# First layer of a four-layer network: where the next image's rows are scaled, and one slot's shift in the layer norm

## Chip, cores and metric

One core of one Trainium2 chip runs the whole program. The metric is the device time of one execution in microseconds (us), lower is better; the number for a kernel is the median over its runs. A profiled execution on the same core gives the trace from which all durations below come. The engines are named as the profile names them: PE (TensorE, with PEld for its weight loads), DVE (VectorE), ACT (ScalarE), POOL (GpSimd), and SP, whose queue issues nearly all DMAs.

## What is computed

The reference is four layers, each added to its input after a group norm. The change is in the first one, a two-dimensional selective scan (4 images of 64 x 64 pixels, 128 channels, inner width 256, 16 states, 4 scan directions). Cut to what matters:

```python
x = x + ss2d(group_norm(x))                      # layer 0, then three other layers
# ss2d:
xh, z = split(x @ in_proj_w.T)                   # 256 channels each
xc = silu(depthwise_conv3x3(xh) + conv_b)        # per image
for k in 4 directions:                           # rows, columns, and both reversed
    delta = softplus(dt_proj(x_proj(xc)));  B, C = x_proj(xc)
    h[t] = exp(delta[t] * A) * h[t-1] + delta[t] * u[t] * B[t]     # 16 states
    y += sum_n h[n] * C[n]
y = layer_norm(y over 256 channels) * silu(z)
out = y @ out_proj_w.T
```

The group norm of the input is a scale and an offset for each channel; the kernel applies them to the rows of the image ahead of the convolution (the scaling that the change moves). The layer norm over the 256 channels is `y * nb + mb` with `nb` the reciprocal deviation and `mb = -mean * nb`.

## The kernel before

**Units and slots.** Layer 0 is one long hand-ordered loop (lines 656 to 779). A unit is one image `b` (4), one direction `k` (4) and one chunk `c` of 512 pixels (8): 128 units. A unit has 16 slots, one for each state `n`: 2048 slots in all. In each slot the program emits, in this order:

- POOL: `dB = du * B` for both halves of the channels (line 699, 128 x 1024)
- DVE: what is filed under `"dve"` for this slot, then for each of the two halves ACT's `dA = exp(delta * A)` (line 704) and DVE's scan over 512 pixels (line 705)
- PE: eight transposes of the scanned `h` of seven slots ago (line 549), and the products of the slot before (line 584); ACT: the copy `hT` out of PSUM (line 559)
- ACT: what is filed under `"act2"` for this slot
- PE and POOL: steps of the next unit by `TABLE`; among them, `delta` on DVE at the head of slots 9 and 11 (line 484), and on POOL `du0` after slot 10's dB and `du1` after slot 12's (line 487)

The order of PE, ACT, DVE and POOL is the order of emission (`tc.manual_schedule`); that of the SP queue is left to the framework. dB has three buffers, so POOL may be up to about two slots ahead of DVE; dA has three PSUM buffers, and the transposes' PSUM tile `pt` has one.

**Work on the side.** While the scans of image `b` run, generators prepare image `b+1` (`before`, line 305) and finish image `b-1` (`after`, line 367). Each `yield` names a kind of piece. At the end of every slot the loop steps pieces whose kind may stand in this slot (`SIDE`) and whose turn has come (`due`). `later(place, f, slots=m)` (line 643) files an operation to be emitted `m` slots on, at `place`.

`before` takes the rows of an image in 8 chunks. For each: `gates` (two products for `z`), then two convolutions `s = 0, 1` of nine matmuls, one in each slot from slot 11 to slot 3 of the next unit. So a chunk takes three units, and I call them A (s = 0 starts in its slot 11), B (s = 0 ends in slot 3, s = 1 starts in slot 11) and C (s = 1 ends in slot 3). The next chunk's rows are loaded at the first matmul of s = 0 and scaled in place by `scaled` (line 324): one ACT instruction, 128 x 10 x 64 values, filed at the sixth matmul of s = 1 for one slot on, which is slot 1 of a C unit. The first chunk of an image is scaled before the loop over the chunks starts. There are 24 scalings (3 images, 8 chunks).

`after` normalises a chunk of an earlier image. For the first two images (`b + 2 < NB`, that is while the scans of images 1 and 2 run) the piece `"t"` emits `nb` on ACT at once, files `mb` (4 columns, DVE, line 390) two slots on, and four operations of 128 x 256 on ACT (`yf`, line 393) two to five slots on. `"t"` may stand in slots 11, 12, 15 and 0, and stands in slot 12 of a B unit in all 16 cases; so `mb` is emitted ahead of slot 14's scans and the four operations at the end of slots 14, 15, 0 and 1. `free_at = slot + 6` holds the next piece, the transposes of the normalised rows, until they are through. For images 2 and 3 DVE does the norm in another way, which isn't touched. Helpers carry the line of the filed call: in the profile `mb`, `yf` and other filed operations stand under L645.

Of the kernel before, what the change touches and what calls it, by code (L numbers as in the profile page):

```python
# [12 lines left out]
AF = mybir.ActivationFunctionType  # L13
ALU = mybir.AluOpType
# [10 lines left out]
NCH = NT // CH  # L25
# [57 lines left out]
def layer0(sh, A, x_in, x_out, scr, ahead):  # L83
# [6 lines left out]
    tc, nc = sh.tc, sh.nc  # L90
    with ExitStack() as ctx:
# [60 lines left out]
        def conv(xn, s, bank, out):  # L152

            for t in range(9):
                yield "c"
                if t == 0:
                    pm = bank("cv")
                dy, dx = divmod(t, 3)
                nc.tensor.matmul(  # L159
                    pm,  # L160
                    lhsT=taps[:, s, t, :],
                    rhs=xn[:, dy : dy + 8, dx : dx + 64],
                    start=(t == 0),
                    stop=(t == 8),
                )
            out.append(pm)
# [6 lines left out]
        def gates(b, c, v, bank, later, es=(None, None)):  # L173
            for s in range(2):
                yield "z"
                zp = bank("zp")
                nc.tensor.matmul(zp, lhsT=w_in[:, 2 + s, :], rhs=v, start=True, stop=True)
                silu(zp, 0.0, 0.0, scr(f"z{b % 3}")[s, :, c * CH : (c + 1) * CH], later, (("act0", 2), ("act0", 3), 4), es[s])
# [126 lines left out]
        def before(b, bank, later):  # L305

            st = small.tile([P, NCH, 6], F32, name="gn_st")
            for c in range(NCH):  # L310
                yield "l"
                t = tmp.tile([P, CH], F32, name="xs", tag="t2", bufs=4)
                nc.sync.dma_start(t.rearrange("p (h w) -> p h w", w=64), A["x_t"][b, :, 8 * c + 1 : 8 * c + 9, 1:65])
                yield "s"
                later("dve", nc.vector.bn_stats, st[:, c, :], t)
            yield "m"
            s_, o_ = sh.group_scale(st, psm, small, "m", exp_rstd)

            def load(c):
                xn = tmp.tile([P, 10, 66], F32, name="xn", bufs=3)  # L320
                nc.sync.dma_start(xn, A["x_t"][b, :, 8 * c : 8 * c + 10, :])
                return xn

            def scaled(xn, c, r0, r1):
                inner = xn[:, max(r0, int(c == 0)) : min(r1, 10 - int(c == NCH - 1)), 1:65]
                nc.scalar.activation(inner, inner, AF.Identity, scale=s_, bias=o_)

            yield "l"
            ahead = load(0)
            yield "x"  # L330
            later("act2", scaled, ahead, 0, 0, 10)
            for c in range(NCH):
                xn = ahead
                yield from gates(b, c, xn[:, 1:9, 1:65], bank, later)
                for s in range(2):
                    for t, piece in enumerate(conv(xn, s, bank, out := [])):
                        yield piece
                        if c < NCH - 1 and (s, t) == (0, 0):
                            ahead = load(c + 1)
                        if c < NCH - 1 and s == 1 and t == 5:  # L340
                            later("act2", scaled, ahead, c + 1, 0, 10)
                    grown(b, c, s, out[0], later)

        def silu(v, bias, minus, dst, later, wait, e=None):
# [22 lines left out]
        def after(b, st, later, bands):  # L367

            for c in bands:
                yield "l"  # L370
                rows = slice(c * CH, (c + 1) * CH)
                if kept:
                    y = kept.pop()
                else:
                    y = tmp.tile([P, 4, 2 * P], F32, name="yf", tag="t4", bufs=4)
                    nc.sync.dma_start(y, tiles(scr(f"y2{b % 2}")[rows, :]))
                z = tmp.tile([P, 2, CH], F32, name="zf", tag="t4", bufs=4)
                nc.sync.dma_start(z, scr(f"z{b % 3}")[:, :, rows].rearrange("s p t -> p s t"))
                mv = small.tile([P, 4, 2], F32, name="ln_mv")
                for q in range(4):  # L380
                    nc.vector.bn_aggr(mv[:, q, :], st[:, 4 * c + q])

                rs = small.tile([P, 4], F32, name="ln_r")
                later("act1", nc.scalar.activation, rs, mv[:, :, 1], AF.Ln, bias=sh.eps5)
                if b + 2 < NB:
                    yield "t"
                    nb = small.tile([P, 4], F32, name="nb")
                    nc.scalar.activation(nb, rs, AF.Exp, scale=-0.5)
                    mb = small.tile([P, 4], F32, name="mb")
                    later("dve", nc.vector.scalar_tensor_tensor, mb, mv[:, :, 0], -1.0, nb, ALU.mult, ALU.mult, slots=2)  # L390
                    for q in range(4):
                        norm = dict(scale=nb[:, q : q + 1], bias=mb[:, q : q + 1])
                        later("act2", nc.scalar.activation, y[:, q, :], y[:, q, :], AF.Identity, slots=2 + q, **norm)
                else:
                    yield "n"

                    nb = spare("nb")[:, 0:4]
                    nc.scalar.activation(nb, rs, AF.Exp, scale=-0.5)
                    for q in range(4):
                        later("dve", normed, y[:, q, :], mv[:, q, 0:1], nb[:, q : q + 1])  # L400
                yg = tmp.tile([P, 2, CH], F32, name="yg", bufs=2)
                for s in range(2):
                    yield "m"
                    pt = spare("pg")
                    for q in range(4):
                        nc.tensor.transpose(pt[:, q * P : (q + 1) * P], y[:, q, s * P : (s + 1) * P], sh.ident)
                    norm = dict(scale=on_w[:, s : s + 1], bias=on_b[:, s : s + 1])
                    later("act0", nc.scalar.activation, yg[:, s, :], pt, AF.Identity, **norm)
                yield "f"
                xr = tmp.tile([P, 4, DM], F32, name="xr", tag="t2", bufs=4)  # L410
                nc.sync.dma_start(xr, tiles(x_in(b)[rows, :]))
                if b < NB - 1 or c > 2:
                    yield "g"
                nc.gpsimd.tensor_tensor(yg, yg, z, ALU.mult)
                if b + 2 < NB:
                    yield "o"
                    op = psy.tile([P, 2, 2 * P], F32, name=f"yT{int(not rev)}").rearrange("p r d -> p (r d)")
                else:
                    yield "m"
                    op = spare("op")  # L420
                op = op.rearrange("p (q d) -> p q d", q=4)
                for q in range(4):
                    for s in range(2):
                        nc.tensor.matmul(
                            op[:, q, :], lhsT=yg[:, s, q * P : (q + 1) * P], rhs=w_out[:, s, :], start=(s == 0), stop=(s == 1)
                        )
                later("dve", residual, b, rows, xr, op, slots=2)
# [134 lines left out]
        def products(G, q, hT):  # L562
# [68 lines left out]
            c={11},  # L631
            g={7},
            s={11, 12, 13, 14, 15, 0, 1, 2, 3},
            t={11, 12, 15, 0},
            o={8},
            f=(),
            l=(),
# [3 lines left out]
        slot = 0  # L641

        def later(place, f, *a, slots=1, **kw):

            todo.setdefault((slot + slots, place), []).append(lambda: f(*a, **kw))  # L645
# [10 lines left out]
        with tc.manual_schedule(engines=order):  # L656
# [4 lines left out]
            for i, (b, k, c) in enumerate(units):  # L661
# [25 lines left out]
                for n in range(NS):  # L687
                    slot = NS * i + n
                    g, q = divmod(n, 4)
# [39 lines left out]
                    if n == 10:  # L729
                        y = unit["y"] = tmp.tile([P, 4, 2 * P], F32, name="y", tag="t4", bufs=4)  # L730
# [15 lines left out]
                        d.step()  # L746
                    for d in sides:
                        if d.need == "t" and n in SIDE["t"] and d.due(slot) and (inside or not any(o.taps for o in sides)):
                            d.free_at = slot + 6
                            d.step()  # L750
                        if d.need == "o" and n in SIDE["o"] and d.due(slot - 8):
                            d.step()
                        if d.need == "s" and n in SIDE["s"] and d.due(slot):
                            d.step()
                        if d.need in ("f", "l") and d.due(slot):
                            if d.need == "l":
                                d.free_at = slot + 3
                            d.step()
# [1455 lines left out]
```

## Time and profile before

| What | Value |
|---|---|
| median of 3 runs (lowest, highest) | 7645.87 us (7638.12, 7647.14) |
| the profiled execution: time | 7645.85 us |
| its span, first to last instruction | 7644.1 us |
| first scan to last scan of layer 0 | 112.8 to 5591.8 us, 2048 slots of 2.68 us |
| scan, L705 (DVE) | 4096 of 1266 ns |
| dB, L699 (POOL) | 2048 of 2387 ns |
| dA, L704 (ACT) | 4096 of 696 ns |
| hT, L559 (ACT) | 2048 of 1016 ns |
| scaling, L326 (ACT) | 24, median 924 ns |
| mb, L645 (DVE) | 16, median 1432 ns |
| yf, L645 (ACT) | 64, median 603 ns |

How to read it: a row of the profile names the line, the engine, the operation, what it writes and reads with sizes, the count, and the mean time of one. Consecutive instructions of DVE and ACT overlap by about 0.1 us, so that the distance from start to start, not the duration, is what one costs its engine. In a time line the first two columns are start and length in us, and "[0.32 <-PE pt L549]" means that the engine sat idle for 0.32 us before it and that PE's write of pt released it.

### The profile page before, as it was taken

To read this page: it belongs to the slowest core of one execution; us is meant where nothing else is said; L and a number is where in the kernel's file an instruction comes from. 1 tells how busy PE (TensorE), PEld (TensorE's weight loads), DVE (VectorE), ACT (ScalarE), POOL (GpSimd) and SP (SyncE) were. 2 spreads that over 40 slices of the span, in tenths; PEclk is the share of its full clock that TensorE was granted. 3 is DMA by queue.
4 is the path that set the end of the run, shared out by engine and by line. 5 is a ranking of instruction groups with operands and counts; after the bars stand their busy time and mean duration, and the time that the engine had idled before them with its cause. 6 is when DMAs were issued, how large, how long until landed. Compare 5 with 4: busy or idle time off the path is not lost.

```text
span 7644.1 us, 140402 instructions
## 1 busy us (share of the span) xinstructions
PE 6293.8 (82%) x52604; PEld 3973.6 (52%) x52604; DVE 6715.7 (88%) x7999; ACT 6135.0 (80%) x9771; POOL 5691.9 (74%) x2688
## 2 busy tenths in 40 slices
PE   7888888778898877888887777787789978686889
PEld 3554444444455544445554444454467756464556
DVE  7999999999999999999999999999956655656678
ACT  7999999999999999999999999999943323324667
POOL 4999999999999999999999999999920024123233
PEclk8999999999999999999999999999999988788999
DMA  6656566546667554565756445555533241331332
GB/s 181 171 177 176 182 175 180 171 154 178 198 180 195 184 179 160 167 196 178 183 191 180 165 169 180 179 185 174 190 92 73 59 120 46 83 99 46 102 95 82
DMA packets 1328925, 1160.66 MB, mean 152 GB/s; under 512 B 718709, under 2 KB 1119697, under 8 KB 1261298
## 3 DMA queue, kind: packets, MB, share of 16 engines
q1 hardware_dynamic: 1323970, 1149.24, 50.4%
q8 instruction: 414, 6.78, 0.4%
q10 hardware_dynamic: 4272, 2.43, 0.1%
q14 instruction: 269, 2.20, 0.1%
HBM read 958.19 MB, written 189.21 MB: 150 GB/s over the span
## 4 chain that ended last, share of the span: by engine, by line
ACT 36%; PE 31%; DVE 18%; issue 8%; POOL 3%; DMA 2%; SPq 1%; ACTq 0%; DVEq 0%; POOLq 0%
ACT hT L559 14%; ACT dA L704 14%; DVE h L705 12%; PE pt L549 5%; PE cv L159 3%; POOL dB L699 3%; PE yT L584 3%; PE pf L939 2%; PE po L952 1%; ACT e L645 1%; ACT delta L478 1%; PE yT L458 1%; PE pz L1183 1%; PE pt L1892 1%; ACT delta L481 1%
## 5 line engine op out<-in xcount | busy, mean ns | idle before, releaser
L705 DVE TENSOR_TENSOR_SCAN h<-dA,state,dB 128x512 f32<-128x512 f32 x4096 | 4927.0, 1266 | 120.7 <-ACT dA L704 72.4
L699 POOL TENSOR_TENSOR dB<-du,Bb 128x1024 f32<-128x1024 f32 x2048 | 4816.5, 2387 | 152.3 <-DVE h L705 118.2
L549 PE MATMUL pt<-ident,h 128*128 128x128 f32 x16384 | 2216.7, 278 | 859.2 <-ACT hT L559 833.8
L704 ACT ACTIVATE dA<-delta,A_neg 128x512 f32<-128x512 f32 x4096 | 2765.5, 696 | 102.7 <-DVE h L705 77.0
L549 PEld LDWEIGHTS pt<-ident,h 128*128 128x128 f32 x16384 | 1802.7, 141 | 1917.7 <-ACT hT L559 1700.5
L559 ACT COPY hT<-pt 128x1024 f32<-128x1024 f32 x2048 | 2080.7, 1016 | 125.5 <-PE pt L549 105.9
L584 PE MATMUL yT<-hT,W 128*32 128x256 f32 x16384 | 1378.6, 409 | 4.3 <-DVE xr L433 3.5
L584 PEld LDWEIGHTS yT<-hT,W 128*32 128x32 f32 x16384 | 456.2, 150 | 346.3 <-issue 324.3
L159 PE MATMUL cv<-xn,taps 128*128 128x512 f32 x936 | 527.1, 645 | 2.7 <-DVE delta L484 2.6
L1183 POOL TENSOR_TENSOR xg<-xg,so 128x1024 f32<-128x1024 f32 x16 | 39.3, 2469 | 622.8 <-PE pu L1183 622.2
L1930 POOL TENSOR_TENSOR S<-S,sm 128x784 f32<-128x784 f32 x128 | 191.1, 1493 | 416.3 <-DVE sm L1928 250.0
L487 POOL TENSOR_TENSOR du<-delta,u 128x512 f32<-128x512 f32 x256 | 327.8, 1281 | 163.6 <-DVE delta L484 162.2
L475 PE MATMUL dp<-xd,w_dt 65*128 65x512 f32 x512 | 288.7, 646 | 33.8 <-DVE delta L484 23.7
L458 PE MATMUL yT<-u,w_x 128*48 128x512 f32 x508 | 244.4, 604 | 21.3 <-DVE y L600 20.1
L1937 ACT ACTIVATE S<-S,mx 128x196 f32<-128x196 f32 x512 | 227.9, 448 | 33.2 <-DVE mx L1964 32.7
L159 PEld LDWEIGHTS cv<-xn,taps 128*128 128x128 f32 x936 | 139.2, 188 | 180.5 <-issue 160.4
L940 ACT ACTIVATE h<-pf,b 128x512 f32<-128x512 f32 x128 | 87.6, 687 | 118.8 <-PE pf L939 100.5
L484 DVE SCALAR_TENSOR_TENSOR delta<-delta,dp 128x512 f32<-128x512 f32 x256 | 169.7, 663 | 3.2 <-ACT delta L481 1.0
L1183 POOL TENSOR_TENSOR WX<-wr,Xs 128x544 f32<-128x544 f32 x40 | 59.3, 1483 | 149.1 <-issue 63.4
L1892 PE MATMUL pt<-ident,S 128*98 128x128 f32 x1024 | 165.6, 286 | 3.5 <-POOL S L1930 2.0
L481 ACT ACTIVATE delta<-delta 128x512 f32<-128x512 f32 x256 | 164.5, 643 | 0.0
L478 ACT ACTIVATE delta<-dp 128x512 f32<-128x512 f32 x256 | 152.3, 595 | 10.4 <-PE dp L475 9.2
(381 smaller groups left out, 6921.7 us busy)
## 6 DMA issues: line engine op xcount, KB each, us to landing
Bb<-l_B SPq DMA_DIRECT2D x512, 1024.0 KB
W<-l_W SPq DMA_DIRECT2D x512, 256.0 KB
l_y<-y SPq DMA_DIRECT2D x127, 512.0 KB
u<-l_xr SPq DMA_DIRECT2D x64, 512.0 KB
u<-l_xw SPq DMA_DIRECT2D x64, 512.0 KB
y<-l_y SPq DMA_DIRECT2D x56, 512.0 KB
V<-l_v SPq DMA_DIRECT2D x512, 49.0 KB
y<-l_y SPq DMA_DIRECT2D x80, 256.0 KB
```

The source lines that it names most:

```text
L159: nc.tensor.matmul(pm, lhsT=taps[:, s, t, :], rhs=xn[:, dy : dy + 8, dx : dx + 64], start=(t == 0), stop=(t == 8),)
L458: nc.tensor.matmul(bank["x"], lhsT=w_x[:, s, k, :], rhs=u[:, s, :], start=(s == 0), stop=(s == 1))
L475: nc.tensor.matmul(bank[s], lhsT=w_dt[:, k, s * P : (s + 1) * P], rhs=xd, start=True, stop=True)
L481: nc.scalar.activation(delta[:, s, :], delta[:, s, :], AF.Ln, bias=1.0)
L487: nc.gpsimd.tensor_tensor(du[:, s, :], delta[:, s, :], u[:, s, :], ALU.mult)
L549: nc.tensor.transpose(pt[:, j, s, :], G["h"][:, s, t0 : t0 + 32, :].rearrange("p t n -> p (t n)"), sh.ident)
L559: return lambda: nc.scalar.copy(hT, pt.rearrange("p j s d -> p j (s d)"))
L584: nc.tensor.matmul(U["yT"][e][32 * jo : 32 * jo + 32, qo % 2, :], lhsT=U["Ws"][G["g"]][:, :, 4 * q + j], rhs=hT[:, j, :], start=((e, jo) n ...
L699: nc.gpsimd.tensor_tensor(dB, du, B_now[:, q : q + 1, :].to_broadcast([P, 2, CH]), ALU.mult)
L704: nc.scalar.activation(dA, delta[:, s, :], AF.Exp, scale=A_neg[:, k, s, n : n + 1])
L705: nc.vector.tensor_tensor_scan(h[:, s, :, q], dA, dB[:, s, :], state[:, s, n : n + 1], ALU.mult, ALU.add)
L1892: nc.tensor.transpose(pt[:, half, hp, :], U["S"][:, e, hp, 98 * half : 98 * half + 98], sh.ident)
```

## The change

The scaling of rows becomes a `tensor_scalar` (multiply, then add) on POOL, and for all chunks but the first it is filed at the last matmul of s = 0 for five slots on: slot 8 of a B unit, emitted on POOL's queue between the dB of slot 8 and that of slot 9. `mb` is filed three slots after `"t"` in place of two (ahead of slot 15's scans), and the four `yf` operations three to six slots after it (slots 15, 0, 1 and 2). `"t"` may stand in slot 12 alone, and the piece after it waits for seven slots.

```diff
             def scaled(xn, c, r0, r1):
                 inner = xn[:, max(r0, int(c == 0)) : min(r1, 10 - int(c == NCH - 1)), 1:65]
-                nc.scalar.activation(inner, inner, AF.Identity, scale=s_, bias=o_)
+                nc.gpsimd.tensor_scalar(inner, inner, s_, o_, ALU.mult, ALU.add)
...
-                        if c < NCH - 1 and s == 1 and t == 5:
-                            later("act2", scaled, ahead, c + 1, 0, 10)
+                        if c < NCH - 1 and s == 0 and t == 8:
+                            later("act2", scaled, ahead, c + 1, 0, 10, slots=5)
...
-                    later("dve", nc.vector.scalar_tensor_tensor, mb, mv[:, :, 0], -1.0, nb, ALU.mult, ALU.mult, slots=2)
+                    later("dve", nc.vector.scalar_tensor_tensor, mb, mv[:, :, 0], -1.0, nb, ALU.mult, ALU.mult, slots=3)
                     for q in range(4):
                         norm = dict(scale=nb[:, q : q + 1], bias=mb[:, q : q + 1])
-                        later("act2", nc.scalar.activation, y[:, q, :], y[:, q, :], AF.Identity, slots=2 + q, **norm)
+                        later("act2", nc.scalar.activation, y[:, q, :], y[:, q, :], AF.Identity, slots=3 + q, **norm)
...
-            t={11, 12, 15, 0},
+            t={12},
...
-                            d.free_at = slot + 6
+                            d.free_at = slot + 7
```

## The prediction, made before the changed kernel ran

> **What bounds the kernel now.** I read in this order: the page, the busy time by stage, the waits of the stage, and then the time line around the edited instructions. The first layer takes 5.6 of the 7.64 ms, and the edits act only while scans of images 0, 1 and 2 run (about 125 to 4300 us), because only then is a next image prepared (line 326) or an earlier one normalised by ScalarE (lines 386 to 393).
>
> ```profile
> PE 6293.8 (82%) x52604; PEld 3973.6 (52%) x52604; DVE 6715.7 (88%) x7999; ACT 6135.0 (80%) x9771; POOL 5691.9 (74%) x2688
> ```
>
> ```profile
> 500.00:1300.00 800.00, 685.39 (x5220) 388.10 (x5212) 783.55 (x717) 773.98 (x1115) 753.52 (x341) 1.00 0.65 181
> 1700.00:2600.00 900.00, 788.70 (x6023) 458.97 (x6016) 871.57 (x812) 875.98 (x1281) 846.18 (x384) 1.00 0.65 186
> ```
>
> The columns are PE, PEld, DVE, ACT, POOL. In both stages DVE and ACT are 97 to 98% busy and POOL 94%: nobody has idle time to sell, so the question is which of them is late in the slots concerned. The waits between 300 and 5500 us (total, times, longest) say how the engines hold each other:
>
> ```profile
> POOL du L487 <- DVE delta L484: 133.2, 105, 2.1
> ...
> DVE h L705 <- ACT dA L704: 68.4, 141, 1.0
> ...
> DVE h L705 <- POOL dB L699: 17.3, 50, 1.2
> ```
>
> DVE is short of ACT for 68 us at most, hardly ever of POOL; POOL waits 133 us for delta. A slot without side work takes DVE 2.35 us (two scans, started 1.175 us apart) and ACT 2.14 at least (its next start comes 0.62 and 0.61 after the two dA, 0.91 after hT). While a convolution runs (slots 11 to 3) PE has its own round. In the scans of image 0, around one scaling:
>
> ```profile
> 845.43 0.67 PE L584 MATMUL yT<-hT,W 128*32 128x256 f32 x8
> 846.03 1.13 PE L159 MATMUL cv<-xn,taps 128*128 128x512 f32 x2
> 847.00 1.04 PE L549 MATMUL pt<-ident,h 128*128 128x128 f32 x8
> ...
> 849.62 1.09 PE L549 MATMUL pt<-ident,h 128*128 128x128 f32 x8
> ```
>
> ```profile
> 845.59 1.01 ACT L559 COPY hT<-pt 128x1024 f32<-128x1024 f32 x1 [0.32 <-PE pt L549]
> 846.50 0.93 ACT L326 ACTIVATE xn<-xn,gn_o,gn_s 128x640 f32<-128x640 f32 x1
> ```
>
> Transposes start at 844.47, 847.00, 849.62: a round of 2.53 us without a gap, and ACT waits 0.32 for PE in each slot ahead of the scaling. The scaling stops DVE once (0.87 us), but PE's next round comes only 0.09 late (2.62 in place of 2.53). In image 0 a scaling is thus hidden by PE, nearly whole.
>
> **What the Trainium skill says.** "SBUF — State Buffer", Who interferes with whom: a DVE instruction with two SBUF inputs contends with a GpSimd instruction that reads SBUF, one with at most one doesn't. The trace agrees: mb (two SBUF inputs, 4 columns) takes 1200/1432/1985 ns (min, median, max), while the scans, with dA in PSUM, take 1.25 to 1.29 beside POOL. "GPSIMD Engine Reference", Engine selection: one-input work is "roughly line-rate" there. The trace disagrees: the only elementwise tensor_scalar on POOL, with one operation, takes 2.84 us for 1024 columns, longer than dB with two inputs (2.39). "Perfetto Trace Analysis", GPSIMD Engine Instruction: a POOL span is unreliable, start to start is better; those rows start 2.84 apart too.
>
> ```profile
> L1183 POOL TENSOR_SCALAR m<-m,scal x16: 2838/2843/3780, 6461.9 to 6997.1; 128x1024 f32<-128x1024 f32 x16
> ```
>
> **The change, part by part.** In the built program TensorE's order is the same; DVE's differs in the place of 16 mb, ACT's by 24 missing scalings and norms a slot later, POOL's by 24 new instructions. SP issues the same DMAs, 38 of 3875 by one to three places. "t" stepped in slot 12 in all 16 cases before, so the new set {12} moves nothing, and free_at + 7 follows the norms.
>
> *ACT loses the scalings.* A scaling holds ACT for 0.81 (2134.72 to 2135.53 in the pair below). 24 x 0.81 = 19.4 us is the most that can be had. Seven in image 0 and two later have no norm beside them: PE hides them but for about 0.1, so 9 x 0.1 = 0.9. The three first chunks (at 335 us and its like) lie outside a convolution: DVE waits 0.36 behind each, 3 x 0.36 = 1.1. In the other 12 the scaling follows the last of four norms in slot 1, and there ACT, not PE, is last: ACT runs without a gap from mb on, DVE waits 0.72 for it, and PE 0.70.
>
> *Norms and mb a slot later.* I work the pair with mb at 2124.71 through.
>
> ```profile
> 2120.01 4.78 DVE L705 TENSOR_TENSOR_SCAN h<-dA,state,dB 128x512 f32<-128x512 f32 x4
> 2124.71 1.46 DVE L645 SCALAR_TENSOR_TENSOR mb<-ln_mv,nb 128x4 f32<-128x4 f32 x1
> 2126.09 3.62 DVE L705 TENSOR_TENSOR_SCAN h<-dA,state,dB 128x512 f32<-128x512 f32 x3
> ```
>
> mb is held until the running dB ends; dBs follow each other every 2.35 there (2119.07, four in 9.43, the next at 2128.68). Moved, the scans of slot 14 start at 2124.88 (dA plus 0.79), mb issues at 2127.23 and finds the next dB in the same phase, ending 2128.5: slot 15 starts at 2128.46, as before (2128.47). A slot of DVE and a dB of POOL are equally long, so one slot later changes nothing in mb's wait: 0. On ACT, norm 1 now starts at 2128.91 where norm 2 stood (2128.96), because hT in slot 15 still waits for PE; the 0.50 freed in slot 14 is lost. The rest adds up from starts: 0.50 for this norm, three slots with a norm (2.14 + 0.50, less 0.01: 2.63 each), a plain one (2.14) and slot 4 with e (2.79); the dA of slot 5 comes at 2142.23, before at 2142.73. So -0.81 for the scaling, +0.50 for the last norm, which now falls in slot 2, and -0.19 in gaps: 0.50 gained. 12 x 0.50 = 6.0. Four norm groups have no scaling behind them; there only the later norm remains, from DVE-bound to ACT-bound: a loss of 0.33 each, 1.3.
>
> *POOL gains the scalings, ahead of dB of slot 9.* Queued behind each: dB 9, dB 10, du0, then du1 and all dBs; DVE waits for these. The cover:
>
> ```profile
> 2105.18 2.38 POOL L699 TENSOR_TENSOR dB<-du,Bb 128x1024 f32<-128x1024 f32 x1 [0.28 <-DVE h L705]
> 2108.18 2.38 POOL L699 TENSOR_TENSOR dB<-du,Bb 128x1024 f32<-128x1024 f32 x1 [0.63 <-DVE h L705]
> 2111.91 1.28 POOL L487 TENSOR_TENSOR du<-delta,u 128x512 f32<-128x512 f32 x1 [1.34 <-DVE delta L484]
> ```
>
> 0.28 + 0.63 + 1.34 = 2.25 us idle between dB 8 and du0 (over the 21 places: 1.9 to 2.2 mostly, up to 3.5), and du0 can't go earlier, for it waits for delta. dB 9 and dB 10 are two slots early and may slip. Price of the new operation: low 0.84 (POOL's copy of 640), high 2 x 640/1024 x 2.84 = 3.55 (each operation a pass); I take the estimate 640/1024 x 2.84 = 1.8, since both operations go in one pass over one input. 1.8 < 1.9: cost 0. Without that cover each tenth over would delay du0 and all behind it. The first chunks go ahead of a dB that is 4.9 us early (needs 2.4): 0. xn's load was issued 13 slots (34 us) earlier, and the scale exists some slots before: no new wait. SP's swaps: 0, bounded by a slot's slack that W, state and u have, -1 to +3 us.
>
> Sum: 0.9 + 1.1 + 6.0 - 1.3 = 6.7 us. The profiled execution took 7645.85 (span 7644.1), the median of the three runs is 7645.87: 7639.
>
> **Rivals.**
> A. ACT is the bound everywhere, and all of its time comes back: 7646 - 19.4 = 7626. For it: ACT at 97%. Against: the 0.32 waits for PE in image 0.
> B. PE's round hides it in images 1 and 2 too, or the norms cost what the scalings gave: 7645. Against: PE's own 0.70 gap there.
> C. Slower: the two-operation scaling is long on POOL. Over about 2.2 us du0 is late, POOL runs without a gap from there to the lock, so mb is held longer by the same amount (12 times), and in image 0 DVE waits once only 0.3 of spare is used up (dB 13 ends 0.33 ahead of its scan; 0.9 in the others). At 2.6 us: 12 x 0.4 + 7 x 0.35 = 7.3, the gain is gone; at 3.55: 12 x 0.9 + 7 x 1.3 + 14 x 0.45 = 26, less 6.7: 7665. For it: POOL's tensor_scalar is already slow with one operation.
> D. The program isn't what the words say: excluded but for SP's swaps, by the order.
>
> **Numbers.** Forecast 0.62 (own range 7633 to 7645), A 0.13, B 0.10, C 0.15. About 0.2% (15 us) is what a measurement here tells from no change: faster needs 7630.6, which is A and a little more, 0.13; slower needs 7661, the upper half of C, 0.08; the same 0.79. The range leaves out half of A and the upper half of C: 7626 to 7656.
>
> **What would show it.** Right: tensor_scalar on line 326 at 1.7 to 2.0 us; DVE's 0.72 and 0.87 waits for dA after slot 1 gone; the C units (convolution ends, slots 13 to 5 around mb) 0.5 shorter, image 0's slots by 0.1; POOL's wait for delta down by 20 x 1.2 to 1.9; mb still 1.2 to 1.5. Wrong: line 326 over 2.2 us with du late, mb near 2 us or near 0.2, or image 0 gaining 0.8 for each scaling.

## The result, and the profile after

The changed kernel takes 7633.44 us (median of 18 runs, 7626.36 to 7637.06); the kernel before, in 18 runs of the same session, takes 7644.33 (7638.12 to 7651.99). The ratio is 0.9984, with a 95% interval of 0.9978 to 0.9990: a gain of 10.9 us (7.6 to 16.8), 0.14%. The forecast was 7639, a gain of 6.7. The direction is right, the forecast gain is about two fifths too small, and the interval of the gain excludes the 6.7 narrowly. The time lies inside the prediction's own range of 7633 to 7645, but only 0.44 us above its lower end.

The busy line of the page of the kernel after (the profiled execution, span 7631.4 us):

```profile
PE 6292.9 (82%) x52604; PEld 3974.2 (52%) x52604; DVE 6716.9 (88%) x7999; ACT 6113.9 (80%) x9747; POOL 5709.0 (75%) x2712
```

ACT lost 24 instructions and 21.1 us of busy time, POOL gained 24 and 17.1 us. The time fell by about half of what ACT lost. The rows of the two tiles concerned (count, then shortest, median and longest duration in ns, then the first and last start) of the kernel after:

```profile
L326 POOL TENSOR_SCALAR xn<-xn,gn_s,gn_o x24: 821/887/1001, 330.6 to 3867.7; 128x640 f32<-128x640 f32 x18, 128x576 f32<-128x576 f32 x6
L645 DVE SCALAR_TENSOR_TENSOR mb<-ln_mv,nb x16: 776/1112/1961, 1689.3 to 4022.4; 128x4 f32<-128x4 f32 x16
```

The scaling takes 0.89 us on POOL, half of the 1.8 on which I had settled. mb is held a little less long than before (median 1.11 against 1.43). The waits between 300 and 5500 us (total, times, longest), first of the kernel after:

```profile
POOL du L487 <- DVE delta L484: 134.9, 104, 3.8
ACT hT L559 <- PE pt L549: 98.0, 256, 1.2
POOL dB L699 <- DVE h L705: 75.6, 168, 1.6
...
DVE h L705 <- ACT dA L704: 56.8, 149, 0.9
DVE h L705 <- POOL dB L699: 16.8, 49, 1.3
```

and the two of the kernel before that the prediction doesn't show:

```profile
POOL dB L699 <- DVE h L705: 102.8, 196, 1.4
...
ACT hT L559 <- PE pt L549: 85.0, 223, 1.2
```

DVE's wait for ACT fell by 11.6 us, from 68.4 to 56.8, about as much as the kernel gained; its wait for POOL did not rise (17.3 to 16.8). ACT's wait for PE rose from 85.0 to 98.0: part of the freed time is only waited out elsewhere. And POOL's wait for delta is unchanged, where the forecast had it shrink; the wait of dB for a free buffer fell instead, from 102.8 to 75.6.

To find where the time went I took the start of the first scan of each slot in both traces and compared how long the same stretch of slots takes. "Pair" is a B unit with a norm group and the C unit after it, in which ACT scaled before. Every row counts from slot 13 of one unit to slot 5 of the next. Numbers in us, negative is shorter:

| Stretch | Instances | Forecast | Measured, each | Measured, sum |
|---|---|---|---|---|
| pair | 12 | -0.50 | -0.61 (and 0.00 in slots 8 to 13) | -7.0 |
| scaling with no norm beside it (image 0 and two more) | 9 | -0.1 | -0.15 | -1.3 |
| norm group with no scaling behind it | 4 | +0.33 | -0.01 to +0.17 | +0.4 |
| first chunk of an image | 3 | -0.36 | -0.57, -1.83, -0.18 | -2.6 |
| sum | | -6.7 | | -10.4 |

The same stretches in a second profile of the changed kernel (the last run below) sum to -9.7: -7.0, -1.2, +0.45 and -1.9. The row of the first chunks holds a second thing, which the edit doesn't touch: TensorE runs slow in some of the slots just ahead of the scaling (the last section). Counted from slot 0 of the scaling's own unit to slot 5, the three give -0.56, -1.30 and -1.26, -3.1 in all, and -3.1 again in the second profile; the sums then are -11.0 and -10.9. The layers after the first were 2 to 9 us shorter in every later profile than in the one profile of the kernel before, whichever edit was made, so a difference of two spans is not a measure of this edit; the stretches and the medians are.

ACT in the pair that the prediction worked through (start, length), first the fourth norm and the scaling of the kernel before:

```profile
2134.22 0.61 ACT L645 ACTIVATE yf<-yf,mb,nb 128x256 f32<-128x256 f32 x1
2134.72 0.94 ACT L326 ACTIVATE xn<-xn,gn_o,gn_s 128x640 f32<-128x640 f32 x1
2135.53 1.31 ACT L704 ACTIVATE dA<-delta,A_neg 128x512 f32<-128x512 f32 x2
```

then the first and the fourth norm of the kernel after:

```profile
2122.36 1.01 ACT L559 COPY hT<-pt 128x1024 f32<-128x1024 f32 x1 [0.32 <-PE pt L549]
2123.26 0.60 ACT L645 ACTIVATE yf<-yf,mb,nb 128x256 f32<-128x256 f32 x1
...
2131.16 0.60 ACT L645 ACTIVATE yf<-yf,mb,nb 128x256 f32<-128x256 f32 x1
2131.66 1.29 ACT L704 ACTIVATE dA<-delta,A_neg 128x512 f32<-128x512 f32 x2
```

The first norm stands after an hT for which ACT waited 0.32 for PE: most of the 0.50 us freed in slot 14 is lost there (from its dA to the next slot's, slot 15 takes ACT 3.04 in place of 2.63). The fourth norm is followed at once by the next dA; the scaling that stood there is gone. POOL at slot 8 of the same unit:

```profile
2094.45 4.83 POOL L699 TENSOR_TENSOR dB<-du,Bb 128x1024 f32<-128x1024 f32 x2
2099.15 1.00 POOL L326 TENSOR_SCALAR xn<-xn,gn_s,gn_o 128x640 f32<-128x640 f32 x1
2100.00 4.91 POOL L699 TENSOR_TENSOR dB<-du,Bb 128x1024 f32<-128x1024 f32 x2
2106.25 1.29 POOL L487 TENSOR_TENSOR du<-delta,u 128x512 f32<-128x512 f32 x1 [1.34 <-DVE delta L484]
```

Before, POOL idled 0.28 and 0.63 ahead of dB 9 and dB 10 and 1.34 ahead of du0. The scaling (0.85 from its start to the next one's) fills the first two gaps, 0.91 together; du0 still waits 1.34 for delta. This is why the wait for delta did not shrink.

### The profile page after: what moved, and what is told of

The parts are those of the page before. It is cut to its first block, busy times and chain, and to the rows that moved or that the text cites. A ratio compares the mean times of both kernels' runs of the same rounds, so it can differ in the third digit from the quotient of the medians.

```text
span 7631.4 us, 140417 instructions
## 1 busy us (share of the span) xinstructions
PE 6292.9 (82%) x52604; PEld 3974.2 (52%) x52604; DVE 6716.9 (88%) x7999; ACT 6113.9 (80%) x9747; POOL 5709.0 (75%) x2712
## 4 chain that ended last, share of the span: by engine, by line
ACT 36%; PE 32%; DVE 18%; issue 8%; POOL 3%; DMA 2%; SPq 1%; ACTq 0%; DVEq 0%; POOLq 0%
ACT hT L559 14%; ACT dA L704 13%; DVE h L705 11%; PE pt L549 6%; PE cv L159 4%; PE yT L584 3%; POOL dB L699 2%; PE pf L939 2%; ACT e L645 2%; PE po L952 1%; PE yT L458 1%; ACT delta L478 1%; PE pz L1183 1%; PE pu L1183 1%; ACT delta L481 1%
## 5 line engine op out<-in xcount | busy, mean ns | idle before, releaser
L1183 DVE TENSOR_TENSOR WX<-wr,Xs 128x544 f32<-128x544 f32 x88 | 76.9, 890 | 96.9 <-PE pz L1183 64.8
```

Of the source, the lines that this page charges most:

```text
L1183: r = f(*args, **kw)
```

## The experiments

Three theories were to be told apart. The prediction's own: in pairs ACT is last and its instructions can be added up start to start; elsewhere PE's round hides the scaling. A rival on the cause: the gain comes from the shift of the norm, or from where the scaling stands, not from the change of engine. And a rival on the price: POOL's new instruction costs something, so that part of what ACT gives is lost again. The kernel before was timed beside each: its median was 7646.34 us in the session of e1 to e4 and 7646.65 in that of e5 to e8, on another chip.

**e1_pool: the scaling on POOL alone.** The norm and mb stay where they were.

```diff
-                nc.scalar.activation(inner, inner, AF.Identity, scale=s_, bias=o_)
+                nc.gpsimd.tensor_scalar(inner, inner, s_, o_, ALU.mult, ALU.add)
...
-                        if c < NCH - 1 and s == 1 and t == 5:
-                            later("act2", scaled, ahead, c + 1, 0, 10)
+                        if c < NCH - 1 and s == 0 and t == 8:
+                            later("act2", scaled, ahead, c + 1, 0, 10, slots=5)
```

> Scaling on GpSimd in slot 8 alone; mb and the four norm operations stay in slot 14 and 14, 15, 0, 1. My account (ScalarE's time in slots 14 to 4 and TensorE's round set the pair; the shift of the norms costs): from slot 13 of B to slot 5 of C each of the 12 pairs with a norm and a scaling comes out 0.8 us shorter than before (0.6 in the changed kernel), image 0 again by 0.15, groups of norms without a scaling by 0; in all 14 us less than before, 7630, and 3 us less than the changed kernel. Rival (the shift to slot 15 is what makes room for the gain): pairs gain 0.3 or less, 7640.

Measured: 7628.47 us, ratio 0.9977 (0.9968 to 0.9986). The pairs are 0.81 shorter each (sum -9.7), the 0.81 that a scaling holds ACT from its start to the next start. This half alone gains more than the whole change: 0.81 a pair in place of 0.61.

**e2_shift: the norm and mb a slot later alone.** The scaling stays on ACT in slot 1.

```diff
-                    later("dve", nc.vector.scalar_tensor_tensor, mb, mv[:, :, 0], -1.0, nb, ALU.mult, ALU.mult, slots=2)
+                    later("dve", nc.vector.scalar_tensor_tensor, mb, mv[:, :, 0], -1.0, nb, ALU.mult, ALU.mult, slots=3)
...
-                        later("act2", nc.scalar.activation, y[:, q, :], y[:, q, :], AF.Identity, slots=2 + q, **norm)
+                        later("act2", nc.scalar.activation, y[:, q, :], y[:, q, :], AF.Identity, slots=3 + q, **norm)
...
-            t={11, 12, 15, 0},
+            t={12},
...
-                            d.free_at = slot + 6
+                            d.free_at = slot + 7
```

> mb and the norms one slot later alone; the scaling stays on ScalarE in slot 1 of C, now between the third norm and the fourth. My account: nothing of ScalarE's work goes, and the 0.5 us freed in slot 14 is lost to a wait for TensorE: each of the 16 groups comes out 0.2 to 0.4 us longer, 4 to 5 us in all, 7649. Rival (the later slot is worth something by itself): 0.3 us or more shorter for each, 7639.

Measured: 7646.93 us, ratio 1.0003 (0.9995 to 1.0011). In the trace the pairs are longer by 0.18 each (sum +2.1), the four groups without a scaling by -0.02 to +0.25 (sum +0.4): about half of the 4 to 5 us expected. The time can't tell 2.5 us from nothing, the stretches can. -0.81 + 0.18 = -0.63 a pair, and the two together measured -0.61: the two halves add up. The shift gives nothing and costs about 2.5 us. That the shift brings the gain falls.

**e3_act8: the place alone.** The scaling stays on ACT and moves to slot 8 of the B unit.

```diff
-                        if c < NCH - 1 and s == 1 and t == 5:
-                            later("act2", scaled, ahead, c + 1, 0, 10)
+                        if c < NCH - 1 and s == 0 and t == 8:
+                            later("act2", scaled, ahead, c + 1, 0, 10, slots=5)
```

> The scaling moved to slot 8 of B but left on ScalarE; norms as before. If the engine is what matters (my account): ScalarE has no gap in slots 7 to 10, so each of 21 scalings costs there 0.5 to 0.8 us (slots 8 to 13 of B), and slot 1 gives 0.8 back in 12 and 0.15 in 9: between 0 and 5 us slower than before, 7646 to 7651. If the place is what matters: as fast as the changed kernel, 7633.

Measured: 7644.63 us, ratio 0.9998 (0.9990 to 1.0006). In the pairs slots 8 to 13 are a median of 0.49 longer (0.0 to 1.2) and the stretch after them 0.85 shorter; in image 0 and its like, slots 8 to 13 are 0.76 longer and only 0.12 comes back. Over all 21 the loss of 11.5 us and the gain of 11.1 nearly cancel. ACT and DVE of this run at slot 8 of an image 0 unit, then DVE of the kernel before at the same place:

```profile
827.13 0.93 ACT L326 ACTIVATE xn<-xn,gn_o,gn_s 128x640 f32<-128x640 f32 x1
827.95 1.30 ACT L704 ACTIVATE dA<-delta,A_neg 128x512 f32<-128x512 f32 x2
```

```profile
827.40 0.66 DVE L484 SCALAR_TENSOR_TENSOR delta<-delta,dp 128x512 f32<-128x512 f32 x1
828.74 4.81 DVE L705 TENSOR_TENSOR_SCAN h<-dA,state,dB 128x512 f32<-128x512 f32 x4 [0.68 <-ACT dA L704]
```

```profile
824.11 0.66 DVE L484 SCALAR_TENSOR_TENSOR delta<-delta,dp 128x512 f32<-128x512 f32 x1
824.69 4.80 DVE L705 TENSOR_TENSOR_SCAN h<-dA,state,dB 128x512 f32<-128x512 f32 x4
```

No convolution runs in these slots, PE's round is not the limit, and DVE waits 0.68 for the dA behind the scaling. The same instruction on the same engine costs 0.15 under PE's round in slot 1 of image 0 and 0.76 here.

**e6_slot1: the engine alone.** POOL scales in slot 1 of the C unit, the place that ACT had.

```diff
-                nc.scalar.activation(inner, inner, AF.Identity, scale=s_, bias=o_)
+                nc.gpsimd.tensor_scalar(inner, inner, s_, o_, ALU.mult, ALU.add)
```

> GpSimd scales, but where ScalarE did: slot 1 of C, ahead of dB of slot 2; norms as before. dB of slot 2 is 4.4 us ahead of its scan in image 0 and 5.5 behind a norm, and needs 2.4, so 0.87 has room (my account): as with GpSimd's scaling in slot 8, 7628, the pairs 0.8 shorter. If the slot matters: the dBs of slots 2 and 3 come late, VectorE waits 0.3 to 0.9 us in up to 21 units, 7635 to 7645.

Measured: 7629.64 us, ratio 0.9979 (0.9970 to 0.9988); pairs -0.81 each, image 0 -0.14. It equals e1 in the pairs, in image 0 and in the norm groups, and in the first chunks counted from slot 0 (-3.1 against -3.2). The engine matters; on POOL, slot 8 is no better than slot 1. That the place brings the gain falls.

**e7_none: no scaling on any engine.** The function's body is left out, so images 1 to 3 are convolved without the group norm's scale and offset; everything else is the kernel before.

```diff
-                nc.scalar.activation(inner, inner, AF.Identity, scale=s_, bias=o_)
+                pass
```

> The scaling of the next image's rows is left out altogether on every engine (images 1 to 3 are convolved unscaled), norms as before. If GpSimd's 24 operations are free (my account): the same as with GpSimd's scaling alone within 3 us, 7628, pairs 0.8 shorter. If they cost anything on GpSimd's queue or through its lock: shorter by that, up to 24 x 0.87 = 21 us, 7607.

Measured: 7631.01 us, ratio 0.9981 (0.9974 to 0.9989). Pairs -0.80, image 0 -0.15 each, first chunks -2.8 together (-3.3 from slot 0). This is the most that taking the scaling off ACT can give, and e1 gives the same: on POOL the scaling costs nothing that can be measured. The rival on the price falls, for a scaling of 0.89 us. ACT and PE of this run in slots 1 to 3 of an image 0 unit, where the prediction showed the kernel before:

```profile
844.91 1.01 ACT L559 COPY hT<-pt 128x1024 f32<-128x1024 f32 x1 [0.31 <-PE pt L549]
...
847.44 1.01 ACT L559 COPY hT<-pt 128x1024 f32<-128x1024 f32 x1 [0.31 <-PE pt L549]
...
849.97 1.01 ACT L559 COPY hT<-pt 128x1024 f32<-128x1024 f32 x1 [0.32 <-PE pt L549]
```

```profile
843.78 1.04 PE L549 MATMUL pt<-ident,h 128*128 128x128 f32 x8
...
846.31 1.04 PE L549 MATMUL pt<-ident,h 128*128 128x128 f32 x8
...
848.84 1.04 PE L549 MATMUL pt<-ident,h 128*128 128x128 f32 x8
```

The hT of slot 2 of the kernel before, the first one after the scaling, waits for nothing:

```profile
848.56 1.01 ACT L559 COPY hT<-pt 128x1024 f32<-128x1024 f32 x1
```

With no scaling ACT waits for PE in slots 2 and 3 too, 0.31 and 0.32, and the transposes come every 2.53 us. Of the 0.81 taken off ACT all but 0.15 goes into waiting for PE.

**e4_long: a long scaling on POOL.** The changed kernel, with three more passes of "times 1 plus 0" over the same rows. At 817.65 us, for one, the scaling and its passes hold POOL for 3.36 us until the next dB starts, in place of 0.84.

```diff
                 nc.gpsimd.tensor_scalar(inner, inner, s_, o_, ALU.mult, ALU.add)
+                for _ in range(3):
+                    nc.gpsimd.tensor_scalar(inner, inner, 1.0, 0.0, ALU.mult, ALU.add)
```

> The changed kernel, with each scaling on GpSimd followed by three more passes over the same rows (times 1, plus 0), so that it takes 4 x 0.87 = 3.5 us in place of 0.87; the result is the same. My account (rival C of the prediction): the cover ahead of du0 is 1.9 to 2.25 us, so du0 comes 1.3 to 1.6 late in 21 units; image 0's slot 13 comes 1.0 to 1.3 later, the others' 0.4 to 0.6, and mb is held longer by up to 0.9; some 15 to 25 us over the changed kernel, 7648 to 7658. If GpSimd's queue has room that the trace doesn't show: as the changed kernel, 7633.

Measured: 7651.98 us, ratio 1.0005 (0.9997 to 1.0013): all of the gain is lost, 18 us against the changed kernel. In five of the seven units of image 0 slot 13 comes 0.9 to 1.1 us later, since du0 is late, and by slot 5 of the next unit all of it has come back: PE's round hides it, net -0.16. In the pairs it stays: a median of -0.15 in place of -0.61, and five of the twelve are 1.5 to 3.5 us longer than before the change. The row of mb of this run, and DVE and POOL around one of the five (two added lines shift all numbers by two):

```profile
L647 DVE SCALAR_TENSOR_TENSOR mb<-ln_mv,nb x16: 1124/1818/4521, 1691.8 to 4039.9; 128x4 f32<-128x4 f32 x16
```

```profile
3507.49 7.30 DVE L707 TENSOR_TENSOR_SCAN h<-dA,state,dB 128x512 f32<-128x512 f32 x6
3514.71 4.52 DVE L647 SCALAR_TENSOR_TENSOR mb<-ln_mv,nb 128x4 f32<-128x4 f32 x1
```

```profile
3507.54 11.67 POOL L701 TENSOR_TENSOR dB<-du,Bb 128x1024 f32<-128x1024 f32 x5
3521.74 4.73 POOL L701 TENSOR_TENSOR dB<-du,Bb 128x1024 f32<-128x1024 f32 x2 [2.54 <-DVE h L707]
```

The five dB follow each other every 2.33 us, so the fourth starts at about 3514.55 and the fifth ends at 3519.2. mb, four columns wide, issues 0.16 after the fourth starts and ends with the fifth: it sat through both. Then POOL idles 2.54, because DVE, held by mb, has not freed a buffer.

**e5_mbpool: e1, with mb on POOL too.** Two small POOL operations do what the DVE one did.

```diff
-                    later("dve", nc.vector.scalar_tensor_tensor, mb, mv[:, :, 0], -1.0, nb, ALU.mult, ALU.mult, slots=2)
+                    later("dve", nc.gpsimd.tensor_tensor, mb, mv[:, :, 0], nb, ALU.mult, slots=2)
+                    later("dve", nc.gpsimd.tensor_scalar, mb, mb, -1.0, None, ALU.mult, slots=2)
```

> GpSimd alone scales in slot 8 (norms in their old slots), and mb too is made on GpSimd, by two operations of 4 columns ahead of slot 14's scans, so that nothing on VectorE has two SBUF inputs there. If ScalarE's time and TensorE's round set the pair (my account), the 1.2 us that mb is held are hidden but for 0.2 to 0.3: pairs 1.0 to 1.1 shorter than before (0.81 without this), groups of norms alone 0.3 to 0.8 shorter, in all 4 us under the kernel with GpSimd's scaling alone, 7624. If the held mb stops the kernel by its own length: 16 x 1.2 = 19 us under it, 7609.

Measured: 7623.15 us, ratio 0.9973 (0.9961 to 0.9984), the best of all. DVE where mb stood, in the pair of before (the scan's line moves from 705 to 706 by the added line):

```profile
2113.72 9.67 DVE L706 TENSOR_TENSOR_SCAN h<-dA,state,dB 128x512 f32<-128x512 f32 x8
2123.68 2.46 DVE L706 TENSOR_TENSOR_SCAN h<-dA,state,dB 128x512 f32<-128x512 f32 x2 [0.28 <-ACT dA L705]
2126.29 2.46 DVE L706 TENSOR_TENSOR_SCAN h<-dA,state,dB 128x512 f32<-128x512 f32 x2 [0.16 <-issue]
2128.94 2.46 DVE L706 TENSOR_TENSOR_SCAN h<-dA,state,dB 128x512 f32<-128x512 f32 x2 [0.18 <-ACT dA L705]
```

The hold is gone, and DVE waits for dA instead: the pairs are -0.81 each, exactly as in e1, though 1.2 to 1.4 us of hold was taken out of each. ACT with its norms sets the length of a pair; DVE's hold lies beside it. So the expectation of 1.0 to 1.1 a pair failed, and its 7624 came near for another reason. Only in the first norm group of an image, where the hold was about 2 us and no scaling stands, does it give 0.53 and 0.43. In the trace e5 is thus about 1 us better than e1; the medians differ by 5.3, across two sessions and within what the two intervals allow. Whether more than that 1 us is real stays open.

**e8_after: the changed kernel once more**, in the second session, for a second trace of it and as a yardstick for the runs beside it.

> The changed kernel again, on the same chip as these: 7633, some 5 us slower than with GpSimd's scaling alone, for the later norms (12 x 0.2 and 4 x 0.1 in the scans, the rest is the spread of runs).

Measured: 7634.38 us, ratio 0.9984 (0.9977 to 0.9990), the first result again, with the stretches given above.

## Why the prediction was right, and which terms were off

The mechanism stood: ACT is last in the pairs, PE's round hides the scaling in image 0, and the whole is 0.1 to 0.2%. That the time fell inside the range is in part luck, though: all four sums of the forecast were off to the same side (three gains too small, the one cost too large), and 7633.44 is 0.44 us from the range's end. Term by term:

- *Pairs, 12 x 0.50 = 6.0; measured a median of 0.61, and 7.0 in all.* The scaling's 0.81 is right to the hundredth (e1, e6, e7). The shift of the norm was priced at +0.31 and costs +0.18 (e2). Here the mechanism held and the size of one term was off.
- *Image 0 and its like, 9 x 0.1 = 0.9; measured 0.15 each, 1.3.* PE hides 0.66 of 0.81, as the 0.32 wait for PE had told. Rival A, with ACT the bound everywhere, falls to e7: with no scaling at all image 0 gives 0.15 for each and not 0.81. The times alone would not settle it: 7631.01 is above A's 7626, but A's 19.4 us are a ratio of 0.9975, inside e7's interval.
- *Norm groups without a scaling, +1.3; measured +0.4.* The last group of an image shows +0.16 and +0.17, half the forecast of 0.33. The first group (mb at 1691.1 and 3075.4 us) shows -0.01 and +0.10, and the +0.10 stands in e1, e3 and e7 too, where no norm moved; these two stand in slot 12 of an A unit, not of a B unit as the section on the kernel before has it for all 16. Over-priced.
- *First chunks, 3 x 0.36 = 1.1; measured 1.9 to 2.8 from slot 13 on (after, its second trace, e1, e7), and 3.1 to 3.3 from slot 0 on.* This is the most under-priced term. The 0.36 was read at 335 us, in image 0, where 0.5 is saved, and carried over to the two others, which save 1.2 to 1.6 each. There the product for `z` from the scaled rows (`zp`) comes right behind the scaling: PE waits 1.32 for it, and ACT, which reads `zp` after one more dA, 0.63 for PE. In image 0 `zp` comes a slot later and waits for nothing. DVE shows four gaps of 0.37, 0.47, 0.31 and 0.19, 1.34 together. PE, ACT and DVE of the kernel before in image 1:

```profile
1615.76 1.13 PE L177 MATMUL zp<-xn,w_in 128*128 128x512 f32 x2 [1.32 <-ACT xn L326]
```

```profile
1616.93 0.60 ACT L645 ACTIVATE e<-zp 128x512 f32<-128x512 f32 x1 [0.63 <-PE zp L177]
```

```profile
1616.39 1.28 DVE L705 TENSOR_TENSOR_SCAN h<-dA,state,dB 128x512 f32<-128x512 f32 x1 [0.37 <-ACT dA L704]
1618.14 1.28 DVE L705 TENSOR_TENSOR_SCAN h<-dA,state,dB 128x512 f32<-128x512 f32 x1 [0.47 <-ACT dA L704]
```

PE and ACT of the kernel after at the same place, without a wait:

```profile
1611.45 1.13 PE L177 MATMUL zp<-xn,w_in 128*128 128x512 f32 x2
```

```profile
1612.61 0.60 ACT L645 ACTIVATE e<-zp 128x512 f32<-128x512 f32 x1
```

- *POOL's price, 1.8; measured 0.89.* The estimate scaled a tensor_scalar of the last layer (2.84 us for 1024 columns) by columns; its own lower bound of 0.84 was the right neighbour. The cost of 0 that was drawn from it holds, but with a price half of the one it was argued from, where 1.8 against 1.9 of cover would have been close: the "roughly line-rate" of one-input work in the Trainium skill's "GPSIMD Engine Reference", Engine selection, which I had set aside on account of that row, fits this operation (0.85 us for 640 columns from start to start) and not that one. What makes that row slow was not tried; DVE is not it, for two of its 16, at 6492.5 and 6980.3 us, take 2.84 us while DVE runs nothing.
- *POOL's wait for delta down by 24 to 38 us; measured 133.2 to 134.9.* A failed sign. It followed from 1.8 us, which would have eaten into the 1.34 ahead of du0 (by 0.9 at the place shown, some 19 us over 21 places, so that 24 to 38 was too much even then); 0.85 fits into the 0.28 + 0.63 ahead of dB 9 and 10.
- *mb's wait, 0.* Nearly right: the median is 1.11 against 1.43 us (the sign named was 1.2 to 1.5), and e5 shows that in pairs even the whole of it is worth nothing.
- *Rival C.* Its price did not arise. Given such a price (e4), it ends slower as it said: on a line through its two points (7646 at 2.6 us, 7665 at 3.55) a hold of 3.36 gives 7661, and 7652 was measured. But it had the loss in the wrong places. It charged image 0 with 0.35 to 1.3 a unit, and there PE gives it all back by slot 5. In the pairs it had mb held longer by what POOL is late; in fact mb was held for 3.5 to 4.5 us in five of twelve, the same five that came out longer, and the other seven were still up to 0.6 shorter than before the change. The Trainium skill's "SBUF — State Buffer", Summary: rules for kernel authors, has a DVE instruction with two SBUF inputs that issues second blocked until the GpSimd instruction finishes. So it was for all 16 mb of the kernel before; in e4 five of 16 were held through two dB that follow each other without a gap. The distance doesn't decide: of the four mb that issued 0.16 to 0.22 after a dB's start three were held through two and one through one, and of the eight that issued 1.0 to 1.3 after, two through two. What does stays open.

The table's stretches sum to 10.4 us of the measured 10.9, and in the second trace to 9.7 of 12.3; the rest lies inside the interval of about 4.6 either way.

**A better version** follows from this: leave the norm and mb where they were and move only the scaling (e1, 7628.47), and mb to POOL too if wanted (e5, 7623.15). Both beat the kernel before with intervals clear of 1. Against the changed kernel e1's and e5's intervals overlap its own, and the lead of e1 rests on the 0.20 a pair seen in the traces. In the session in which e5, e6 and the changed kernel were timed together, the medians are 7623.15, 7629.64 and 7634.38, and four of e5's six runs are faster than all 21 of the changed kernel.

## What to carry to other kernels

Before crediting an edit with an engine's freed time, ask slot by slot which engine's round is the longest there: the same 0.81 us instruction was worth 0.81 beside the norms, 0.76 ahead of a dA with no convolution running, and 0.15 under TensorE's round. Leaving the work out altogether (e7) gives the ceiling in one run, and each half of a two-part change alone shows whether the second half pays; here it took back 3.0 of the 10.9 us that the first had given outside the first chunks. An engine with short idle gaps can take work for nothing as long as it fits into them: 0.85 us went into 0.91 of gaps ahead of a wait of 1.34. With 3.36 us all of the gain was lost; what lies between was not tried. The loss did not arise in the slots that came late first, which PE's round made good, but in the pairs, where one engine held another.

## What the runs showed that I had not expected

TensorE slows down behind the group norm. In stretches of the kernel before ahead of and right after the norm between images 0 and 1 (start and end, length, busy time and count of PE, PEld, DVE, ACT, POOL, then the granted clock, the DMA share and GB/s):

```profile
1592.00:1597.00 5.00, 3.10 (x32) 1.86 (x30) 5.00 (x6) 5.00 (x9) 5.00 (x3) 1.00 0.03 10
...
1602.00:1605.00 3.00, 3.00 (x18) 1.87 (x17) 1.70 (x3) 2.57 (x6) 2.01 (x1) 0.50 0.58 218
1605.00:1608.00 3.00, 2.92 (x20) 1.79 (x16) 3.00 (x3) 2.15 (x4) 1.95 (x1) 0.50 0.95 340
1608.00:1612.00 4.00, 3.37 (x36) 2.18 (x32) 3.40 (x4) 3.91 (x7) 3.31 (x3) 0.96 0.34 132
```

```profile
1600.76 0.38 PE L72 MATMUL gn_g<-gn_mv,gmat 128*128 128x1 f32 x2 [2.53 <-DVE gn_mv L69]
1601.66 0.58 PE L76 MATMUL gn_g<-gn_d,gmat 128*128 128x1 f32 x2 [0.51 <-DVE gn_d L75]
1602.10 1.95 PE L549 MATMUL pt<-ident,h 128*128 128x128 f32 x8
...
1605.15 1.97 PE L549 MATMUL pt<-ident,h 128*128 128x128 f32 x8
```

PE idles 2.53 and 0.51 us there while DVE works on the statistics, and then has a clock of 0.50 for some 6 us: eight transposes take 1.95 and 1.97 us instead of 1.04 to 1.09. At the same place of the kernel after they took 1.41, 1.63 and then 1.09, and in its second trace 1.11, 1.97 and 1.95. The Trainium skill's "TensorE: Matmul & The Clock Gate", Part 1, names this, a clock halved after an idle window that runs free of the program, so that the number of slow matmuls varies from run to run; the records agree. It explains the scatter of the first chunks, whose stretch from slot 13 on takes in these slots. In image 0 the transposes take 1.95, 1.97 and 1.09 in the kernel before and 1.07, 1.97 and 1.97 in e1 and e7, and slot 14 is 0.76 longer there. From slot 0 on the transposes take 1.03 to 1.10 in all of these traces, and there the stretches agree: what a first chunk gains differs by at most 0.3 us between after, its second trace, e1, e6 and e7. In e2 and e3, which leave it on ACT, it changes by 0.14 at most.
